# Layer 0 of a two-layer convolution block: chains on GpSimd, edges of t from PSUM, shared statistics, and stores of xs on ScalarE's queue

## The chip, the cores and the metric

The kernel runs on one core of one Trainium2 chip. The metric is the device time of one execution in microseconds; the time of a kernel is the median of its runs. The engines are TensorE (PE; its weight loads are shown as PEld), VectorE (DVE), ScalarE (ACT), GpSimd (POOL) and SyncE (SP, which here only issues DMAs).

## The reference

The input x has 4 images of 64 channels and 256 x 256 pixels in float32. Two layers follow one another, each a residual branch on a group norm:

```python
def _L0_conv_ref(x, ...):
    h = _gelu(_conv2d(x, c1_w, ((1, 1), (1, 1))) + c1_b)          # 3x3, 64 -> 64
    h = _c1x1(h, c2_w, c2_b)                                     # 64 -> 128
    xa, k = jnp.split(h, 2, axis=1)
    xs = _conv2d(xa, sh_w, ((0, 0), (1, 1)), groups=C) + sh_b     # three taps along a row
    xs = _gelu(_conv2d(xs, sv_w, ((1, 1), (0, 0)), groups=C) + sv_b)   # three taps down a column
    pooled = xs.mean(axis=(2, 3))
    weights = jax.nn.softmax(pooled @ gate_w.T, axis=1)          # 3 experts, the top 2 are kept in mask
    ...
    for i, (w1, b1, w2, b2, w3, b3) in enumerate(experts):        # ranks 2, 4, 8
        e = _c1x1(_c1x1(k, w2, b2) * _c1x1(xs, w1, b1), w3, b3)
        out = out + e * mask[:, i][:, None, None, None]           # out starts as xs
    return _c1x1(out, proj_w, proj_b)

def _L1_conv_ref(x, ...):
    h = jax.nn.relu(_batchnorm(_conv3x3(x, _quantize_weight(w1), b1)))
    h = _batchnorm(_conv3x3(h, _quantize_weight(w2), b2))
    return jax.nn.relu(h + x)

x = x + _L0_conv_ref(_gn(x), ...)      # layer 0
x = x + _L1_conv_ref(_gn(x), ...)      # layer 1
```

The batch norms take their mean and variance over all four images, so each convolution of layer 1 has to finish before its norm can be applied. The gate of an image needs the mean of xs over the whole image, so an image's output can't begin before its last rows have passed.

## The kernel before, in words

The two halves of the partitions hold 64 channels each of different rows. Layer 0 works on units: one unit is 16 rows of one image, an image has 16 units, and there are 64 units in all. A unit is worked on in stages, spread over several slots. A slot is the stretch in which one unit's convolution is computed, and there are 64 slots and three tail slots.

In slot u the following happens.

- SP loads x of unit u+3. ACT and GpSimd make row differences of x for units u+2 and u+1 (x_four, x_seconds, v_inner, v_outer; lines 526 to 575), which serve as a row transform of the 3x3 convolution.
- PE multiplies unit u's rows into PSUM (ps_c, line 492). ACT copies parts of it out (mc, L605), DVE combines them in eight butterflies (L610 to L629), and ACT applies the Gelu, which gives h (L637).
- For units u-2 and u-1, PE applies the 1x1 convolution and the column taps together into ps_a, of which there is a single buffer. ACT writes t, the middle tap of the row taps with its bias (`front_taps_i`, L677); DVE adds the left and the right tap, both read from PSUM (`front_taps_h`, L683 and L686), and subtracts from the first and the last column what the padding must not contribute (`ends`, L689). ACT applies the second Gelu, which gives xs and its sums for the pooled mean (`front_xs`, L705), and SP stores xs to DRAM (`xs_store`, L710), 0.5 MB each.
- Every second slot, PE makes the low-rank products (`front_k`, `front_q`), DVE multiplies them (`front_low`, L746), and SP stores them right behind it in program order (L747).

Three further streams share the slots. The statistics of image b+1 are gathered while image b is worked on: a piece of the input is loaded (L409), ACT makes its sum and its sum of squares with two activations (`stats_piece`, L432). For image 0, which comes ahead of all slots, half of the pieces go through DVE's bn_stats instead (`stats_group`, L414), and only the other half through ACT. The statistics of image 1 lie in slots 1 to 12, of image 2 in 12 to 27, of image 3 in 28 to 43; a chain of small operations ends them (`stats_end`). When an image's xs is whole, a chain of small operations makes its gate and the weights of the output (`gate`). Then the output of image b is made, beginning three slots after the next image begins: loads of the low-rank products (L822), of xs (L812) and of x (y, L803), PE's product ps_o, DVE's addition to y (L848), its statistics for layer 1 (L853), and the store of y (L861). `out_end` closes them with another chain of small operations.

The order of the work on every engine is written out by hand. `at_slot(u, pos, call)` puts a call into slot u at a position between 0 and 12; the calls of all streams are sorted by slot and position, and each engine runs its instructions in that order. Where a chain is a generator, each place in a list advances it by one `yield`. The calls of the tail slots are mapped by the table TAIL into the first steps of layer 1. All DMAs, whichever engine issues them, take their completion semaphores in turn from the same set.

Layer 1 is a pair of 3x3 convolutions (L295 and what feeds it), with the batch norms between them, and an end loop (L1422 to L1424) that loads, adds and stores the output. The change doesn't touch it.

Of the kernel before, what the change touches and what calls it, by code (L numbers as in the profile page):

```python
# [41 lines left out]
def conv_preact_kernel(ctx: ExitStack, tc: tile.TileContext, io, col128, colset, col64):  # L42
# [96 lines left out]
    end, ends = column("end", 2), column("ends", 2)  # L139
# [34 lines left out]
    def weights():  # L174
# [22 lines left out]
        nc.vector.tensor_scalar(ends, end, sv_sum, None, ALU.mult)  # L197
        for i in range(2):
            o = outer[:, i, :]
            nc.vector.tensor_scalar(o, zeros[:, 0:W], sh_bias, None, ALU.add)  # L200
            nc.vector.tensor_tensor(o[:, 0 : W : W - 1], o[:, 0 : W : W - 1], end, ALU.subtract)
            nc.vector.tensor_scalar(o, o, c128("sv")[:, 2 * i : 2 * i + 1], None, ALU.mult)
# [59 lines left out]
    def combine(mv, n, avg, eps_t, out, name):  # L262
# [6 lines left out]
        nc.vector.tensor_scalar(mean, mean, 1.0 / n, None, ALU.mult)  # L269
        d = stat.tile([P, n], F32, tag="cd", name=f"d_{name}")  # L270
        nc.vector.tensor_scalar(d, mv[:, :, 0], mean, None, ALU.subtract)
        nc.vector.tensor_tensor(d, d, d, ALU.mult)
        nc.vector.tensor_tensor(d, d, mv[:, :, 1], ALU.add)
# [11 lines left out]
    def group_norm(st, avg, out, name):  # L285
# [3 lines left out]
        yield from combine(mv, 1, avg, eps, out, name)  # L289
# [135 lines left out]

    def stats_piece(b, n, i, at_sum=None):
# [7 lines left out]
    def stats_sums(b, mv):  # L434

        s = stat.tile([P, 2], F32, tag="st_sum", name=f"st_sum_{b}")
        n = NCH if b == 0 else 2 * NCH
        nc.vector.tensor_reduce(s, st_x.pop(b)[:, :, 0:n], AX.X, ALU.add)
        nc.vector.tensor_scalar(s, s, 1.0 / (n * 2 * GF), None, ALU.mult)
        sq = stat.tile([P, 1], F32, tag="st_sq", name=f"st_sq_{b}")  # L440
        nc.vector.tensor_tensor(sq, s[:, 0:1], s[:, 0:1], ALU.mult)
        nc.vector.tensor_tensor(mv[:, 1:2], s[:, 1:2], sq, ALU.subtract)
        nc.vector.tensor_tensor(mv[:, 0:1], s[:, 0:1], shift_x.pop(b), ALU.subtract)
# [12 lines left out]
    def stats_end(b):  # L456

        own = gn1[b] = stat.tile([P, 3], F32, tag="gn1", name=f"gn1_{b}")
        n = 2 if b == 0 else 1
        mv = stat.tile([P, n, 2], F32, tag=f"mv{n}", name=f"mv_x{b}")  # L460
        if b == 0:
            nc.vector.bn_aggr(mv[:, 1, :], flat(st_g.pop(b)))
        stats_sums(b, mv[:, 0, :])
        yield
        yield from combine(mv, n, c128("avg4"), eps, own, f"x{b}")
        if b == 0:
            scale_weights(b)
        nc.vector.tensor_tensor(gn1[b][:, 2:3], gn1[b][:, 0:1], gn1[b][:, 1:2], ALU.mult)
# [204 lines left out]
    def front_taps_i(u, sub):  # L673
# [3 lines left out]
        nc.scalar.activation(flat(t), flat(ps), AF.Identity, bias=tap_bias, scale=sh[:, 1:2])  # L677

    def front_taps_h(u, sub):

        ps = open_a.pop((u, sub)).rearrange("p a b c -> p (a b) c")
        t = open_t[u, sub]
        nc.vector.scalar_tensor_tensor(  # L683
# [4 lines left out]
        )  # L688
        nc.vector.tensor_tensor(  # L689
            t[:, :, 0 : W : W - 1],  # L690
            t[:, :, 0 : W : W - 1],
            ends.unsqueeze(1).to_broadcast([P, 2 * GP, 2]),
            ALU.subtract,
# [13 lines left out]
    def xs_store(u, sub):  # L707
        b, k = divmod(u, NCH)
        n = 2 * k + sub
        nc.sync.dma_start(xs_d[b][:, n, :], flat(xss[b, n]))  # L710
# [32 lines left out]
    def front_low(b, j):  # L743
# [3 lines left out]
        nc.sync.dma_start(low_d[b][:, j, :], low)  # L747
# [4 lines left out]
    def gate(b):  # L752
# [4 lines left out]
        nc.vector.tensor_scalar(spread, zeros[:, 0:P], psum_t, 1.0 / (H * W), ALU.add, ALU.mult)  # L757
# [9 lines left out]
        nc.vector.tensor_scalar(lg, lg, mx, None, ALU.subtract)  # L767
# [8 lines left out]
        yield  # L776
# [3 lines left out]
        nc.vector.tensor_scalar(beat[:, 3:6], beat[:, 0:3], -1.0, 1.0, ALU.mult, ALU.add)  # L780
        keep = stat.tile([P, 3], F32, tag="keep", name=f"keep_{b}")
        for e, (i, j) in enumerate(((3, 4), (0, 5), (1, 2))):
            nc.vector.tensor_tensor(keep[:, e : e + 1], beat[:, i : i + 1], beat[:, j : j + 1], ALU.mult)
        nc.vector.tensor_scalar(keep, keep, -1.0, 1.0, ALU.mult, ALU.add)
        nc.vector.tensor_tensor(keep, g[:, 0:3], keep, ALU.mult)
        yield
# [3 lines left out]
        nc.vector.tensor_tensor(pick[:, 0:4, :], keep.unsqueeze(1).to_broadcast([P, 4, 3]), of, ALU.mult)  # L790
        nc.vector.tensor_tensor(pick[:, 4, :], keep, pb3, ALU.mult)
        row = stat.tile([P, 5], F32, tag="row", name=f"row_{b}")
        nc.vector.tensor_reduce(row, pick, AX.X, ALU.add)
        wm[b] = lstat.tile([P, 4, C], F32, tag="wm", name=f"wm_{b}")
        nc.vector.tensor_tensor(
# [3 lines left out]
        nc.vector.tensor_tensor(out_bias[b], row[:, 4:5], c128("proj_b"), ALU.add)  # L799
# [68 lines left out]
    def out_end(b):  # L868
        gn2[b] = const.tile([P, 3], F32, name=f"gn2_{b}")
        yield from group_norm(st_y.pop(b), c128("avg4"), gn2[b][:, 0:2], f"y{b}")  # L870
        nc.vector.tensor_scalar(gn2[b][:, 2:3], gn2[b][:, 0:1], gn2[b][:, 1:2], -1.0, ALU.mult, ALU.mult)
# [110 lines left out]
    with tc.manual_schedule(engines={mybir.EngineType.Activation}):  # L982
        for k in range(NCH):
# [3 lines left out]
            for i in range({0: 0, NCH - 1: 4}.get(k, 2)):  # L987
                stats_group(0, 2 * k - 2 + i if k else 0, k, i)
            for n in range({0: 2, NCH - 1: 0}.get(k, 1)):
                for i in range(2):  # L990
                    stats_piece(0, 2 * k + n if k == 0 else 2 * k + 1, i, k + n if k == 0 else k + 1)
# [20 lines left out]
    def at_each(places, chain):  # L1012
# [9 lines left out]
        (0, 1.15): (0, 1.15), (0, 1.55): (0, 1.55), (0, 4.7): (0, 4.7), (0, 2): (0, 2), (0, 2.2): (0, 2.2),  # L1022
        (0, 4): (0, 13.2), (0, 4.15): (0, 13.3), (0, 5.2): (0, 13.4), (0, 5.3): (0, 13.5), (0, 8.6): (1, 13.9),
        (0, 9.2): (3, 13.25), (0, 7): (2, 13.2), (0, 7.2): (2, 13.25), (0, 8): (3, 13.1), (0, 9): (3, 13.2), (0, 9.1): (3, 13.3),
        (1, 1.15): (3, 13.4), (1, 1.55): (3, 13.5), (1, 4.7): (4, 13.9), (1, 2): (5, 13.2), (1, 2.2): (5, 13.25),
        (1, 4): (6, 13.2), (1, 4.15): (6, 13.3), (1, 5.2): (6, 13.4), (1, 5.3): (6, 13.5), (1, 8.6): (7, 13.9),
        (1, 8): (8, 13.2), (1, 8.1): (8, 13.3),
# [513 lines left out]
```

## Time and profile before

| | |
|---|---|
| median of 3 runs | 3026.77 us (3007.64 to 3039.1) |
| profiled execution | 3016.92 us |
| its span | 3015.1 us, mean granted TensorE clock 0.913 |
| busy, share of the span | PE 78%, DVE 82%, ACT 68%, POOL 56% |
| layer 0, about | 0 to 1330 us |
| layer 1's two convolutions, about | 1331 to 2564 us |
| end loop, about | 2564 to 3015 us |
| bytes read and written in DRAM | 573.74 MB and 338.17 MB, 302 GB/s over the span |

The lines of a group read: line, engine, operation, output <- inputs by the program's names, shapes, count, then busy time and mean ns of one, then the idle time of the engine just before these instructions and what ended it. A wait line reads: the engine and the line that waits, what released it, the time waited in total, how often, and the longest. A queue with the letter q behind its engine, as SPq, is the stream of DMA issues of that engine. Idle time of an engine that isn't the limit costs nothing.

### The profile page before, as it was taken

What the parts mean: (1) busy time and instruction counts of PE and PEld (TensorE: products, weight loads), DVE (VectorE), ACT (ScalarE), POOL (GpSimd) and SP (SyncE); (2) the same over time, 40 slices, a digit from 0 to 9 for tenths busy, and PEclk for the clock granted to TensorE, in tenths of its full rate; (3) what the DMA queues carried; (4) which work ended last, traced back from release to release, by engine and by line L of the source; (5) the groups of instructions that cost most, each with busy time, mean ns of one, the idle gap of its engine ahead of it and who ended that gap; (6) DMA issues with size and microseconds to landing.
All of it is one profiled execution on the core that took longest, in us unless ns stands there. A gap on an engine that the chain in (4) does not pass through costs nothing.

```text
span 3015.1 us, 52987 instructions
## 1 busy us (share of the span) xinstructions
PE 2357.4 (78%) x21576; PEld 1503.4 (50%) x21576; DVE 2478.0 (82%) x2793; ACT 2054.8 (68%) x2274; POOL 1676.3 (56%) x1210
## 2 busy tenths in 40 slices
PE   1898899998999999988999999989999999000000
PEld 1444444444544445546666667867888888000000
DVE  5678688888888999968988989979999898876665
ACT  6898887787876555557667667868888887422222
POOL 5888887776877778744445546635555555000000
PEclk9999999999999999998999999989999999555555
DMA  8565479999999879848999897746777764899999
GB/s 345 191 249 224 184 259 376 350 342 352 336 343 324 303 288 326 293 147 310 366 356 352 321 345 300 267 178 255 263 266 264 265 232 144 351 411 409 421 427 409
DMA packets 135572, 915.35 MB, mean 304 GB/s; under 512 B 14944, under 2 KB 15712, under 8 KB 40608
## 3 DMA queue, kind: packets, MB, share of 16 engines
q1 hardware_dynamic: 126112, 844.85, 75.0%
q10 hardware_dynamic: 9216, 67.11, 5.5%
q8 instruction: 169, 2.77, 0.4%
q14 instruction: 75, 0.61, 0.1%
HBM read 573.74 MB, written 338.17 MB: 302 GB/s over the span
## 4 chain that ended last, share of the span: by engine, by line
PE 28%; DMA 18%; DVE 5%; issue 2%; ACT 1%; POOL 0%; SPq 0%; DVEq 0%; ACTq 0%; POOLq 0%
PE ps_h L295 18%; PE ps_h2m L295 6%; DMA y_end<-y_d 5%; DMA h<-h_d 4%; DMA out<-h 4%; PE ps_hm L295 3%; DMA y<-in_xp 2%; DVE diff L352 1%; PE ps_o L492 1%; DMA y_d<-y 1%; DVE h L317 1%; DMA h_d<-h 1%; DMA yn<-y_d 1%; DMA xs_in<-xs_d 1%; DVE odd L361 1%
## 5 line engine op out<-in xcount | busy, mean ns | idle before, releaser
L295 PE MATMUL ps_h<-diff,w_q 128*128 128x512 f32 x3072 | 753.8, 400 | 14.3 <-DVE h L317 13.7
L295 PEld LDWEIGHTS ps_h<-diff,w_q 128*128 128x128 f32 x3072 | 576.6, 189 | 192.1 <-issue 23.7
L492 PE MATMUL ps_c<-v,us 64*64 64x256 f32 x9216 | 544.6, 385 | 42.2 <-DVE ps_c L623 36.4
L342 POOL TENSOR_TENSOR d<-yn 128x1024 f32<-128x1024 f32 x128 | 356.0, 2801 | 305.3 <-DMA yn<-y_d 188.5
L492 PEld LDWEIGHTS ps_c<-v,us 64*64 64x64 f32 x9216 | 361.3, 136 | 200.4 <-DVE ps_c L623 45.6
L342 POOL TENSOR_TENSOR d<-h 128x1024 f32<-128x1024 f32 x127 | 311.9, 2477 | 194.8 <-DVE diff L350 133.4
L492 PE MATMUL ps_a<-h,av 64*64 64x512 f32 x4080 | 386.8, 492 | 34.8 <-DVE t L686 23.9
L317 DVE SCALAR_TENSOR_TENSOR h<-ps_h,scale_w,m 128x1024 f32<-128x1024 f32 x256 | 322.8, 1279 | 76.6 <-PE ps_h L295 53.9
L540 POOL TENSOR_TENSOR x<-x 128x512 f32<-128x512 f32 x256 | 329.9, 1289 | 12.3
L1422 ACT ACTIVATE v<-y_end,shift,gn 128x2048 f32<-128x2048 f32 x64 | 133.8, 2092 | 285.1 <-DMA y_end<-y_d 249.9
L492 PEld LDWEIGHTS ps_a<-h,av 64*64 64x64 f32 x4080 | 154.2, 133 | 302.6 <-issue 195.6
L381 ACT ACTIVATE junk<-h,less_h 128x2048 bf16<-128x2048 f32 (+3 forms) x133 | 256.0, 1925 | 11.1 <-DVE h L317 11.0
L1423 DVE SCALAR_TENSOR_TENSOR h<-h,ss,v 128x2048 f32<-128x2048 f32 x64 | 149.8, 2349 | 126.1 <-ACT v L1422 102.1
L683 DVE SCALAR_TENSOR_TENSOR t<-ps_a,m,t 128x1020 f32<-128x1020 f32 x128 | 163.3, 1276 | 103.1 <-ACT t L677 101.1
L848 DVE SCALAR_TENSOR_TENSOR y<-ps_o,ob,y 128x1024 f32<-128x1024 f32 x128 | 163.7, 1279 | 80.6 <-DMA y<-in_xp 27.4
L677 ACT ACTIVATE t<-ps_a,tap_bias,m 128x1024 f32<-128x1024 f32 x128 | 154.0, 1203 | 97.5 <-PE ps_a L492 96.9
L705 ACT ACTIVATE xs<-t 128x1024 f32<-128x1024 f32 x128 | 134.9, 1054 | 116.8 <-DVE t L689 86.8
L352 DVE SCALAR_TENSOR_TENSOR diff<-d,gn,diff 128x1024 fp32r<-128x1024 f32 x128 | 208.5, 1658 | 0.3 <-ACT diff L345 0.3
L295 PE MATMUL ps_hm<-odd,w_q 128*128 128x512 f32 x768 | 194.0, 402 | 8.6 <-ACT m L311 6.0
L295 PE MATMUL ps_h2m<-odd,w_q 128*128 128x512 f32 x768 | 193.2, 400 | 8.2 <-DVE odd L361 4.4
L345 ACT ACTIVATE diff<-d 128x1024 fp32r<-128x1024 f32 x128 | 135.1, 1055 | 83.4 <-POOL d L342 82.2
L532 POOL TENSOR_TENSOR x<-x,x 128x512 f32<-128x512 f32 x128 | 160.7, 1278 | 43.3 <-ACT x L526 43.3
(226 smaller groups left out, 4306.5 us busy)
## 6 DMA issues: line engine op xcount, KB each, us to landing
x<-in_xc SPq DMA_DIRECT2D x64, 1280.0 KB
h<-h_d SPq DMA_DIRECT2D x64, 1152.0 KB
yn<-y_d SPq DMA_DIRECT2D x60, 1152.0 KB
xs_in<-in_xp SPq DMA_DIRECT2D x64, 1024.0 KB
xs_d<-xs SPq DMA_DIRECT2D x128, 512.0 KB
xs_in<-xs_d SPq DMA_DIRECT2D x64, 1024.0 KB
y<-in_xp SPq DMA_DIRECT2D x64, 1024.0 KB
y_d<-y SPq DMA_DIRECT2D x64, 1024.0 KB
```

Of the source, the lines that this page charges most:

```text
L295: nc.tensor.matmul(ps, wq[w][:, kind, kx, :], t[:, rows, kx : kx + W], start=(j == 0), stop=(j == len(terms) - 1))
L317: nc.vector.scalar_tensor_tensor(h.rearrange("p (e k) w -> p e (k w)", e=2), ps.rearrange("p e k w -> p e (k w)"), w_scale[w], m.unsqueeze ...
L342: engine.tensor_tensor(raw.rearrange("p (g r) w -> p g r w", g=2), *pair, ALU.subtract)
L352: nc.vector.scalar_tensor_tensor(lower, raw, scale, upper.bitcast(F32), ALU.mult, ALU.subtract)
L381: nc.scalar.activation(junk[rows, 0:n], flat(h), AF.Square, bias=less[name][rows], accum_out=total)
L492: last[:] = [nc.tensor.matmul(ps[o, at_out[0] : at_out[1], :], w[i], rhs[i], **flags)]
L532: nc.gpsimd.tensor_tensor(x4[:, j - 1], x_rows(u, j + 2), x4[:, j - 1], ALU.subtract)
L540: nc.gpsimd.tensor_tensor(x[:, r : r + 2], x[:, r + 2 : r + 4], x[:, r : r + 2], ALU.subtract)
L677: nc.scalar.activation(flat(t), flat(ps), AF.Identity, bias=tap_bias, scale=sh[:, 1:2])
L683: nc.vector.scalar_tensor_tensor(t[:, :, 1:W], ps[:, :, 0 : W - 1], sh[:, 0:1], t[:, :, 1:W], ALU.mult, ALU.add)
L848: nc.vector.scalar_tensor_tensor(y, ps.rearrange("p x s w -> p x (s w)"), out_bias[b], y, ALU.add, ALU.add)
L1423: nc.vector.scalar_tensor_tensor(h, h, ss2[:, 0:1], v, ALU.mult, ALU.add)
```

## The change

The change has five parts, all in layer 0.

1. **Edges of t.** ACT writes only the inside columns of t. DVE makes the two edge columns first, from PSUM with a bias of their own (`edge_bias`), and then adds the taps. The subtraction of `ends` is gone.
2. **xs stores.** ACT issues them instead of SP, at other positions: (u, 1.6) and (u, 6.135) in place of (u, 4.7) and (u, 8.6).
3. **low store.** It is separated from `front_low` and put at the end of the odd slots, (u, 11.9), behind the store of y at (u, 8.25).
4. **Small operations.** Those of `stats_end` of images 1 to 3, of `gate` of images 0 to 2 and of `out_end` of images 0 and 1 go from DVE to GpSimd where they can; reductions and reciprocals stay on DVE. The square root and the exponential on ACT stand later in their slot, the gate's chain has one more `yield` and ends one slot later, and the output of an image begins four slots after the next image instead of three.
5. **Statistics of image 1.** They are made as those of image 0: half of the pieces by DVE's bn_stats, half by ACT.

The diff, with repeated places of the same kind left out:

```diff
+        nc.vector.tensor_scalar(edge_bias, ends, -1.0, tap_bias, ALU.mult, ALU.add)
...
-    def combine(mv, n, avg, eps_t, out, name):
+    def combine(mv, n, avg, eps_t, out, name, engine=nc.vector):
...
         nc.vector.tensor_reduce(mean, ps[:, 0:n], AX.X, ALU.add)
-        nc.vector.tensor_scalar(mean, mean, 1.0 / n, None, ALU.mult)
+        engine.tensor_scalar(mean, mean, 1.0 / n, None, ALU.mult)
...
+    HALVED = (0, 1)
+
+    def stats_parts(k):
+
+        groups = [(2 * k - 2 + i if k else 0, k, i) for i in range({0: 0, NCH - 1: 4}.get(k, 2))]
+        pieces = [
+            (2 * k + n if k == 0 else 2 * k + 1, k + n if k == 0 else k + 1)
+            for n in range({0: 2, NCH - 1: 0}.get(k, 1))
+        ]
+        return groups, pieces
...
-        nc.scalar.activation(flat(t), flat(ps), AF.Identity, bias=tap_bias, scale=sh[:, 1:2])
+        inside = slice(1, W - 1)
+        nc.scalar.activation(t[:, :, inside], ps[:, :, inside], AF.Identity, bias=tap_bias, scale=sh[:, 1:2])
...
+        edges = slice(0, W, W - 1)
+        nc.vector.scalar_tensor_tensor(
+            t[:, :, edges], ps[:, :, edges], sh[:, 1:2],
+            edge_bias.unsqueeze(1).to_broadcast([P, 2 * GP, 2]), ALU.mult, ALU.add,
+        )
         nc.vector.scalar_tensor_tensor(
             t[:, :, 1:W], ps[:, :, 0 : W - 1], sh[:, 0:1], t[:, :, 1:W], ALU.mult, ALU.add
         )
...
-        nc.vector.tensor_tensor(
-            t[:, :, 0 : W : W - 1], t[:, :, 0 : W : W - 1],
-            ends.unsqueeze(1).to_broadcast([P, 2 * GP, 2]), ALU.subtract,
-        )
...
-        nc.sync.dma_start(xs_d[b][:, n, :], flat(xss[b, n]))
+        nc.scalar.dma_start(xs_d[b][:, n, :], flat(xss[b, n]))
...
-        nc.sync.dma_start(low_d[b][:, j, :], low)
+        low_of[b, j] = low
+
+    def low_store(b, j):
+        nc.sync.dma_start(low_d[b][:, j, :], low_of.pop((b, j)))
...
+        gate_engine = nc.gpsimd if b < B - 1 else nc.vector
+        gate_engine.tensor_scalar(spread, zeros[:, 0:P], psum_t, 1.0 / (H * W), ALU.add, ALU.mult)
...
-                at_slot(u, 8.6, xs_store, u - 2, 1)
+                at_slot(u, 6.135, xs_store, u - 2, 1)
...
-                at_slot(u + 1, 4.7, xs_store, u - 1, 0)
+                at_slot(u + 1, 1.6, xs_store, u - 1, 0)
...
+                at_slot(u, 11.9, low_store, *divmod(j, NOCT // 4))
...
-                places = (t + 1, 8.3), (t + 2, 1.25), (t + 2, 1.36), (t + 2, 1.52), (t + 2, 6.15), (t + 2, 8.3), (t + 2, 9.06)
+                places = (t + 1, 8.3), (t + 2, 1.25), (t + 2, 1.36), (t + 2, 4.45), (t + 2, 6.15), (t + 2, 8.3), (t + 3, 4.1), (t + 3, 4.9)
...
-            for i in range(2):
+            groups, pieces = stats_parts(k) if b in HALVED else ([], [(2 * k, None), (2 * k + 1, None)])
...
+            for group in groups:
+                s = slots[k] + group[2] // 2 * per / 2
+                at_slot(int(s), 4.1 if s - int(s) < 0.5 else 6.2, stats_group, b, *group)
...
-        t = NCH * (b + 1) + 3
+        t = NCH * (b + 1) + 4
...
-            for place in ((e, 8.3), (e + 1, 1.25), (e + 1, 1.36), (e + 2, 1.25), (e + 2, 1.36), (e + 2, 1.52), (e + 2, 6.15)):
+            for place in ((e + 1, 4.1), (e + 2, 1.25), (e + 2, 1.36), (e + 3, 1.25), (e + 3, 1.36), (e + 3, 4.45), (e + 3, 8.3)):
```

## The prediction

> **What bounds the kernel now.** I read the page's chain first, then the windows cut by stage, then the waits, then groups by form.
>
> ```profile
> PE 28%; DMA 18%; DVE 5%; issue 2%; ACT 1%; POOL 0%; SPq 0%; DVEq 0%; ACTq 0%; POOLq 0%
> ```
>
> The chain ends in layer 1, which is the same instructions in both kernels (1331 to 3015 us). So the question is when the front ends, at about 1330 us in the profiled execution. Its windows (columns: stretch and length, then busy us and count of PE, PEld, DVE, ACT, POOL; granted clock; DMA share; GB/s):
>
> ```profile
> 76.00:372.00 296.00, 256.40 (x3676) 136.16 (x3669) 207.87 (x267) 259.34 (x379) 250.42 (x228) 0.97 0.58 211
> 372.00:712.00 340.00, 318.45 (x4445) 163.41 (x4446) 285.69 (x372) 265.54 (x375) 264.54 (x245) 0.99 0.90 334
> 712.00:1055.00 343.00, 323.89 (x4512) 167.68 (x4512) 302.64 (x404) 242.19 (x326) 261.37 (x240) 1.00 0.92 329
> 1118.00:1267.00 149.00, 148.64 (x2120) 77.23 (x2116) 134.58 (x166) 86.92 (x109) 122.66 (x114) 1.00 0.88 313
> ```
>
> Four stages with different limits. Image 0 (first row, about 16 slots): ACT, PE and POOL are each 85 to 88% busy and DMA is at 0.58, so three engines hand work round and ACT is the fullest. Images 1 and 2: DMA at 0.90 to 0.92 with PE at 94%. Last row: PE 148.64 of 149 us; nothing but fewer matmuls shortens it.
>
> From the events at which DMAs complete I worked out more. A 1 MB DMA has 16 completions; 12 come 5 to 9 us after its issue and four, always the same, after 13 to 20 us. From slot 18 to slot 61 those four follow one another without a gap (2.47 us per MB, 1.24 per half). So these slots are paced by four DMA rings: 40.3 to 40.7 us per pair of slots while statistics loads run. Slot lengths, from Gelu to Gelu at L637: slots 2 to 12 mean 17.9, 13 to 18 mean 19.5, 20 to 43 mean 20.3, 44 to 51 between 18.7 and 25.6, 52 to 60 about 18.5.
>
> The queue of SP and the engines wait as follows (waited for: us in total, times, longest):
>
> ```profile
> SPq L803 <- DMA y_d<-y: 372.6, 56, 13.1
> SPq L747 <- DVE k L746: 225.1, 30, 12.4
> SPq L710 <- ACT xs L705: 183.6, 33, 11.5
> SPq L409 <- DMA xs_in<-xs_d: 21.8, 11, 2.1
> ```
> ```profile
> DVE t L683 <- ACT t L677: 101.1, 72, 9.2
> ACT xs L705 <- DVE t L689: 86.8, 50, 3.9
> DVE y L848 <- DMA y<-in_xp: 27.4, 9, 4.5
> PE ps_a L492 <- DVE t L686: 23.9, 27, 3.3
> ```
>
> SP stands 409 us at the stores of xs and low, with loads queued behind. The fourth line is of another kind: a load waiting for a store that it has no data from. The kernel's DMAs share eight completion semaphores in turn, so each issue waits until the DMA eight issues earlier has landed.
>
> The groups that the change touches (times, busy us, mean ns):
>
> ```profile
> L432 ACT ACTIVATE xs_in<-xs_in,shift 128x1024 f32<-128x1024 f32 x112 | 127.1, 1135 | 1.8 <-DVE shift L423 1.8
> L432 ACT ACTIVATE xs_in<-xs_in 128x1024 f32<-128x1024 f32 x112 | 117.9, 1053 | 1.7
> L689 DVE TENSOR_TENSOR t<-t,ends 128x8 f32<-128x8 f32 x128 | 55.2, 431 | 4.4
> L414 DVE BATCH_NORM_STATS2 st_x<-xs_in 128x6 f32<-128x512 f32 x32 | 20.5, 684 | 18.9 <-DMA xs_in<-in_xp 18.9
> ```
>
> **What the skill says.** "SBUF — State Buffer", Who interferes with whom: a DVE instruction with two SBUF inputs contends with a GpSimd instruction that reads SBUF; with at most one, outside the two-port modes, it doesn't. The trace agrees: L689 (both inputs SBUF) takes 172 to 1329 ns, median 269, while L686 (one input PSUM) takes 1280. "GPSIMD Engine Reference", Elementwise — side-by-side cycle accounting: dispatch is about 156 ns on DVE and more hops on GpSimd; POOL's smallest operation here, the L485 memset, takes 0.10 us and its 128x4 and 64x256 ones 278 and 920 ns, so I price a moved operation at 0.3 us. "DMA: Bandwidth & Descriptors", Issuing engines are not separate DMA queues: DMAs of any engine interleave on the same 16 DMA engines, and a second issuer saves only issuing time. Nothing here shows stores from ACT in the front; ACT's store of h_d in layer 1 costs 0.33 us beside a running activation.
>
> **The change part by part.**
>
> *Image 1's statistics.* ACT loses 16 pieces of two activations: 16 x (1.135 + 1.053) = 35 us, plus up to 6 of readouts. DVE gains 32 x 0.684 = 21.9 us. This lies in slots 1 to 12, where DVE has 30% free. ACT's load falls by 35/12 = 2.9 us a slot; behind it stand POOL (4 x 1.29 + 2 x 1.28 + 6 x 1.285 = 15.4, with the memset 15.6 us a slot) and PE (about 15.5). I take 17.9 to 16.2: 12 x 1.7 = -20. Bounds: -28 (down to 15.6), and -8 if DVE's extra 1.8 us a slot stands ahead of the taps.
>
> *Edges of t.* 128 subtractions of mean 431 ns (55.2 us) go; 128 edge operations from PSUM of about 0.18 us come ahead of the two taps. ACT's xs starts 0.25 us earlier, worth something where that wait ends a slot, in slots 13 to 19: -2. Against it, the single PSUM bank of ps_a comes free 0.18 us later, on 27 waits of PE: 5 us at most, all hidden in ring-paced slots.
>
> *xs stores on ACT.* 128 issues of 0.33 us, mostly beside the activation ahead: at nothing, 42 us of ACT if the cover goes. Bytes stay the same. SP no longer waits 184 us for xs, so its loads, and the y_d store behind low, go earlier. In slots 20 to 43 the rings are full, so earlier issues only queue: -4 (from -25, if turn-around gaps fill, to +20, if ACT is held). The new wait: each store on ACT waits for the DMA eight issues before. Counting the new order, in odd slots the first store waits for the y load of the slot before and the second for its y_d store; in even slots both wait for xs stores. Queued behind on ACT are the copies mc, h and t, for which DVE's butterflies and PE wait.
>
> *low store.* Moved behind y_d: SP's 225 us at low no longer hold y_d, so y_d lands some 4 us earlier every second slot, and the y load with it. That and the free SP act where slots stall above PE's 18.55 us: slots 44 to 51, excess 15.1 us in sum, of which I take -9 (-3 to -13). At the end of the front (1305 to 1375) SP stands at xs stores from 1323 to 1345 and at low until 1357, ahead of layer 1's loads; PE has 20 us idle from 1300 to 1400. I take -4 (-10 to +5).
>
> *Small operations on GpSimd.* 9 per later image, about 12 per gate, 5 per out_end: some 70 operations, 0.3 us each, 20 us of POOL, spread where POOL is 75% busy and rings pace. DVE loses its collisions (0.9 to 1.1 us for L757, L767, L775, L780). Nothing, +-5; one chain's end comes a few us later and out of an image starts one slot later. Out then runs into one more tail slot: +2.
>
> Sum: -20 - 2 - 4 - 9 - 4 + 2 = -37 against the profiled 3016.92 us (span 3015.1), so 2980. The four executions known average 3022.6 us, the median of runs is 3026.77; carrying 3022.6 - 37, I give **2985**.
>
> **The rivals.**
>
> *B: given back.* Image 0 ends 20 us sooner, but out of image 0 and the rings come in at the same pace, and image 0's gain is spent waiting: for: from slot 18 four rings have no gap, and the same bytes have to pass. Against: at slots 0 to 17 they have gaps, so earlier bytes are really earlier. -10: 3012.
>
> *C: ACT held by its own stores.* Place: the first xs store of odd slots, behind the y load's landing, 13 to 20 us after an issue that lies less than a slot (20 us) earlier. For: the slow rings land just then, and SPq L409 shows such a wait at 2 us even with SP's looser order. Against: ACT is 70% busy in those slots and can catch up. Price: it decides from 37/21 = 1.8 us per odd slot lost over some 21 odd slots; at 3.3 us it costs 69, a sum of +32: 3055.
>
> *D: faster still.* A second issuer keeps the rings fed, filling turn-arounds and bringing slots 20 to 43 near 19: another -30: 2955. For: PE's floor is 18.55. Against: no gaps are seen in the four slow rings.
>
> **How the numbers follow.** Forecast 0.50, B 0.27, C 0.15, D 0.08. About 1% (30 us) is what a measurement of this kernel can tell from no change, given runs from 3008 to 3039. Faster by over 1% (below 2996) takes the forecast and D: 0.58; within 1% B: 0.27; slower C: 0.15. The range from 2945 to 3040 takes in the forecast's bounds (stage terms all low give some -80, all high +5), D, B and the near side of C.
>
> **What would show it.** Right: slots 2 to 12 near 16.2 us and ACT's share in 76 to 372 lower by about 35 us of work; wait ACT xs behind L689 gone; SPq no longer at xs; the front ending about 1295; layer 1's length unchanged within 5 us. Wrong: ACT waiting at xs's store line for DMA y or y_d, with h and mc late and PE's gaps at ps_c longer in odd slots (C); slots 20 to 43 longer than 20.3 by what image 0 gained (B). If PE's granted clock in layer 1 differs, that part is no work of the change.

## The result, and the profile after

| | before | after |
|---|---|---|
| median | 3019.15 us (6 runs, 3007.64 to 3039.1) | 2988.34 us (6 runs, 2982.45 to 2997.53) |
| ratio | | 0.9903, 95% interval 0.9884 to 0.9922 |
| span of the profiled execution | 3015.1 us | 2988.7 us |

The forecast was 2985 us, and the median lies within 4 us of it. The stages agree less well: in the two profiled executions those of the table below add up to -20.7 us, where the forecast had -37, and two of its terms were wrong altogether. The rest of this text is mostly about those two.

The lengths of the stages, from the start of the first Gelu of each unit (the h activation, one per slot) in the two traces. An eviction is the step with which DVE takes finished products out of PSUM, and conv1 is layer 1's first convolution; the last column is the end of the front, where the last units of layer 0 and the beginning of conv1 overlap.

| us | to slot 13 | 13 to 19 | 20 to 43 | 44 to 51 | 52 to 62 | slot 63 to 16th eviction of conv1 |
|---|---|---|---|---|---|---|
| before | 237.2 | 135.5 | 486.9 | 163.5 | 204.8 | 118.4 |
| after | 236.0 | 129.9 | 480.2 | 156.6 | 206.3 | 116.6 |
| forecast of the difference | -20 | -2 | -4 | -9 | +2 | -4 |
| measured | -1.2 | -5.6 | -6.7 | -6.9 | +1.5 | -1.8 |

The stretch from the last matmul of the second convolution to the end was 446.0 us before and 440.8 after. It is the same instructions in all 14 kernels of this case, and in the 12 others it lies between 440.0 and 443.6 us but for one at 452.9, with 441.2 in a kernel that differs from the one before in a single part; so I take these 5 us for scatter and not for work of the change. About 21 of the 26.4 us by which the two spans differ are then the change's; the medians differ by 30.8 us.

The windows of the changed kernel, with the columns as in the prediction:

```profile
76.00:372.00 296.00, 254.47 (x3712) 135.96 (x3716) 216.74 (x292) 229.62 (x317) 254.94 (x241) 0.98 0.58 212
372.00:712.00 340.00, 322.76 (x4538) 168.91 (x4534) 280.08 (x363) 272.79 (x383) 274.70 (x272) 0.99 0.92 339
712.00:1055.00 343.00, 325.79 (x4533) 167.16 (x4532) 286.67 (x373) 242.73 (x324) 270.13 (x277) 0.99 0.93 327
```

In the first row ACT went from 259.34 to 229.62 us: the 30 us of relief are there. PE's 254.47 is what it was (256.40), so about the same work took the same time with an idler ACT. In the next two rows PE has 2 to 4 us more busy time in the same stretch and the DMA share rose by 0.01 to 0.02, which fits stages that move faster.

The waits of SP's queue and of the engines in the changed kernel:

```profile
SPq L886 <- DVE y L873: 518.2, 64, 22.8
SPq L828 <- DMA y_d<-y: 275.1, 59, 12.8
SPq L770 <- DVE k L764: 214.0, 31, 37.3
```
```profile
ACT xs L723 <- DVE t L710: 88.4, 51, 3.9
PE ps_a L506 <- DVE t L710: 40.1, 36, 3.4
```

SP no longer waits for xs. It now stands longer at the store of y, for DVE's addition. The same wait in the kernel before:

```profile
SPq L861 <- DVE y L848: 282.4, 42, 22.6
```

The wait at low kept its size (225.1 us before), but it now comes behind the store of y. The y load's wait for that store fell from 372.6 to 275.1 us. The wait of ACT's xs for DVE has a new releaser and the old size (86.8 before): the edges are now ahead of the taps, and ACT waits for the last tap instead. PE's wait for the taps grew from 23.9 to 40.1 us.

The edges themselves, and the statistics:

```profile
L699 DVE SCALAR_TENSOR_TENSOR t<-ps_a,m,edge_bias 128x8 f32<-128x8 f32 x128 | 29.1, 227 | 117.0 <-ACT t L692 116.8
L415 DVE BATCH_NORM_STATS2 st_x<-xs_in 128x6 f32<-128x512 f32 x64 | 40.9, 681 | 19.0 <-DMA xs_in<-in_xp 19.0
```

The edge operation takes 227 ns from PSUM where the SBUF subtraction had a mean of 431. There are 64 bn_stats now, 32 of them for image 1.

### The profile page after: what moved, and what is told of

The parts are those of the page before. It is cut to its first block, busy times and chain, and to the rows that moved or that the text cites. A ratio compares the mean times of both kernels' runs of the same rounds, so it can differ in the third digit from the quotient of the medians.

```text
span 2988.7 us, 52829 instructions
## 1 busy us (share of the span) xinstructions
PE 2351.9 (79%) x21576; PEld 1500.3 (50%) x21576; DVE 2440.1 (82%) x2754; ACT 2024.8 (68%) x2210; POOL 1682.5 (56%) x1283
## 4 chain that ended last, share of the span: by engine, by line
PE 50%; DMA 27%; DVE 10%; POOL 6%; ACT 3%; issue 3%; SPq 0%; ACTq 0%; DVEq 0%; POOLq 0%
PE ps_h L296 19%; PE ps_c L506 8%; PE ps_a L506 6%; PE ps_h2m L296 6%; DMA y<-in_xp 6%; DMA y_d<-y 5%; PE ps_o L506 5%; DMA y_end<-y_d 5%; DMA out<-h 4%; DMA h<-h_d 4%; PE ps_hm L296 3%; POOL x L554 2%; DMA xs_in<-xs_d 2%; DVE y L873 1%; DVE t L707 1%
## 5 line engine op out<-in xcount | busy, mean ns | idle before, releaser
L506 PE MATMUL ps_c<-v,us 64*64 64x256 f32 x9216 | 538.4, 382 | 28.6 <-DVE ps_c L637 23.8
L343 POOL TENSOR_TENSOR d<-yn 128x1024 f32<-128x1024 f32 x128 | 347.8, 2738 | 305.6 <-DMA yn<-y_d 189.8
L506 PE MATMUL ps_a<-h,av 64*64 64x512 f32 x4080 | 388.0, 494 | 55.2 <-DVE t L710 40.1
L692 ACT ACTIVATE t<-ps_a,tap_bias,m 128x1016 f32<-128x1016 f32 x128 | 153.4, 1199 | 128.7 <-PE ps_a L506 99.7
L873 DVE SCALAR_TENSOR_TENSOR y<-ps_o,ob,y 128x1024 f32<-128x1024 f32 x128 | 163.9, 1280 | 74.8 <-PE ps_o L506 26.8
L353 DVE SCALAR_TENSOR_TENSOR diff<-d,gn,diff 128x1024 fp32r<-128x1024 f32 x128 | 192.3, 1531 | 0.5 <-ACT diff L346 0.5
L546 POOL TENSOR_TENSOR x<-x,x 128x512 f32<-128x512 f32 x128 | 160.9, 1280 | 22.2 <-ACT x L540 22.2
L296 PEld LDWEIGHTS ps_h2m<-odd,w_q 128*128 128x128 f32 x768 | 146.3, 191 | 44.5 <-DVE odd L362 5.2
```

The costliest lines, as they stand in the source:

```text
L296: nc.tensor.matmul(ps, wq[w][:, kind, kx, :], t[:, rows, kx : kx + W], start=(j == 0), stop=(j == len(terms) - 1))
L343: engine.tensor_tensor(raw.rearrange("p (g r) w -> p g r w", g=2), *pair, ALU.subtract)
L353: nc.vector.scalar_tensor_tensor(lower, raw, scale, upper.bitcast(F32), ALU.mult, ALU.subtract)
L506: last[:] = [nc.tensor.matmul(ps[o, at_out[0] : at_out[1], :], w[i], rhs[i], **flags)]
L546: nc.gpsimd.tensor_tensor(x4[:, j - 1], x_rows(u, j + 2), x4[:, j - 1], ALU.subtract)
L692: nc.scalar.activation(t[:, :, inside], ps[:, :, inside], AF.Identity, bias=tap_bias, scale=sh[:, 1:2])
```

## The experiments

Twelve kernels ran, in three groups of four. A ratio is against runs of the kernel before in the same group (its median was 3018.91, 3014.01 and 3016.73 us in the three). Multiply a difference of ratios by 3017 for microseconds. The intervals are about +-0.0018 wide, so the difference of two variants is uncertain by some 0.0025, or 8 us; smaller differences are read from the stage table further down or not at all. A stage is read from one profile, and slots 20 to 43 scatter by several us there.

### Statistics of image 1 back on ScalarE

```diff
-    HALVED = (0, 1)
+    HALVED = (0,)
```

> The changed kernel with image 1's statistics all on ScalarE again (the halving for image 0 alone); the other four parts stay. My prediction gave this part -20 us: by it the time is 3008 and slots 2 to 12 go from 16.2 to 17.9 us. The trace of the changed kernel says otherwise: its slots 2 to 12 are still about 17.8 us, because the two bn_stats that DVE now makes (1.2 to 1.4 us) stand in the loop PE ps_c, ACT mc, four DVE butterflies, two bn_stats, DVE edges and taps, PE ps_a, PE ps_k, PE ps_c, of 17.7 us. By that theory what ACT gains DVE's loop takes, and undoing the part costs 0 to 5 us: 2988 to 2993. Rival: GpSimd bounds these slots, whatever ACT and DVE do: the same 0 here.

Measured: 2984.88 us, ratio 0.9885 (0.9867 to 0.9903). Undoing the part costs nothing that can be seen (the ratio is 0.0018 lower, not told apart from 0); a loss of 20 us would have been a ratio of 0.9969, far outside the interval. ACT was busy 186.52 of 200 us between 110 and 310 here and 154.92 in the changed kernel, and the stage to slot 13 is 235.9 against 236.0 us. The -20 is refuted.

### bn_stats behind the taps

```diff
-                at_slot(int(s), 4.1 if s - int(s) < 0.5 else 6.2, stats_group, b, *group)
+                at_slot(int(s), 5.25 if s - int(s) < 0.5 else 6.2, stats_group, b, *group)
```

> The changed kernel with the first two of each slot's bn_stats for image 1 placed behind the taps of t (position 5.25) instead of ahead of them (4.1). Loop theory: the loop shortens by the 1.2 us that the trace's chain shows for them, slots 2 to 12 go from 17.7 to 16.5, and the time by some 12 us to 2976. Rival (GpSimd, 15.6 us of work and a wait of about 2 us for its tick in each slot, or PE is the bound): slots stay at 17.7 and the time at 2988.

Measured: 2986.42 us, ratio 0.9891 (0.9873 to 0.991). Slots 2 to 10 are at 17.1 to 17.9 us and the stage at 235.4. The loop theory in this form fell: the bn_stats had been on the chain, but taking them off it saved 0.6 us in thirteen slots, not 12. The chain then ran through GpSimd (v, v, v, 2.0 us idle, tick), which made GpSimd the next suspect.

### GpSimd's tick one operation later

The tick is a memset on GpSimd that waits for one group of PE's products in ps_a and releases the next.

```diff
-                at_slot(u, 2.2, divide)
+                at_slot(u, 2.35 if u < UNITS else 2.2, divide)
...
-                at_slot(int(s), 4.1 if s - int(s) < 0.5 else 6.2, stats_group, b, *group)
+                at_slot(int(s), 5.25 if s - int(s) < 0.5 else 6.2, stats_group, b, *group)
```

> The changed kernel with bn_stats behind the taps (as in the run with position 5.25) and with GpSimd's tick of the first half of a slot (L499, a memset that orders two groups of PE's products in ps_a) one GpSimd operation later: position 2.35 instead of 2.2. Theory now: slots 2 to 12 are GpSimd's, 15.4 us of work and 2.0 us in which it stands at the tick for PE's products, 17.4 in sum; with the tick behind v (1.22 us) it stands 0.8 us and a slot takes 16.5 us, the length of the PE, DVE loop. Image 0 gets shorter by some 10 us and the time falls to 2976. Rival: what image 0 gains is spent in the ring-paced slots that follow: slots 2 to 12 at 16.5 but 2986 as before. Second rival: PE waits longer for the later tick and the slots stay at 17.4.

Measured: 2983.96 us, ratio 0.9901 (0.9883 to 0.9919). GpSimd's idle time ahead of the tick fell from 2.0 to 0.8 us as expected, and slots 2 to 10 stayed at 17.1 to 17.7. The chain of waits of this run helps to see why; the longest pieces of one period (start, length, what):

```profile
138.87 1.30 POOL v L581
140.25 1.27 POOL v L582
141.53 1.25 POOL v L584
142.78 0.79 issue
143.59 0.11 POOL tick L499
143.74 0.71 PE ps_a L506 x8
144.47 1.21 ACT t L692
145.70 0.24 DVE t L699
145.97 1.29 DVE t L707
147.29 1.29 DVE t L710
148.58 0.14 issue
148.72 2.38 PE ps_a L506 x24
151.10 1.88 PE ps_k L737 x32
152.97 0.59 PE ps_a L506 x8
153.56 1.35 PE ps_c L506 x22
154.99 1.29 POOL v L580
156.28 1.31 POOL v L581
```

From v to v it is 156.28 - 138.87 = 17.41 us, and all four engines appear. One piece has to be read with care, the 0.79 us of "issue" ahead of the tick. The waits of this run from 110 to 310 us put GpSimd's idle time there down to PE:

```profile
POOL tick L499 <- PE ps_a L506: 11.6, 10, 5.6
```

PE was at work without a break from 136.0 to 143.5 us (ps_c, then ps_a), and the tick waited for the end of this. So the v operations run beside PE, and only the tick itself, 0.11 us, is on the loop that ends last. Moving it shortened GpSimd's idle time and nothing else, and the theory that these slots are GpSimd's falls.

What remains is PE's own row and what it waits for. From 143.74 to 148.72 us PE makes the last products of one half, ACT writes t from them, and DVE adds the edges and the taps; the single buffer of ps_a keeps PE from the next half until then, and it has only 2.8 us of ps_c to do meanwhile. The next half, ps_k and ps_a follow without a gap, then ps_c. In these 17.41 us PE works 15.7 and stands 0.9 us for the taps, 0.6 for DVE's butterflies (ps_c) and 0.3 for the tick. None of these three waits ends with an operation of the statistics.

The same waits of PE from 110 to 310 us, first before, then in the changed kernel:

```profile
PE ps_c L492 <- DVE ps_c L623: 15.9, 12, 2.2
PE ps_a L492 <- POOL tick L485: 3.6, 13, 0.4
PE ps_a L492 <- DVE t L686: 1.8, 3, 0.7
```
```profile
PE ps_a L506 <- DVE t L710: 14.0, 12, 1.9
PE ps_c L506 <- DVE ps_c L637: 7.2, 12, 0.7
PE ps_a L506 <- POOL tick L499: 2.8, 11, 0.3
```

With 30 us less on ACT, PE's wait for the butterflies fell from 15.9 to 7.2 us, and its wait for the taps rose from 1.8 to 14.0. In sum PE waited 21.3 us before and 24.0 after. In the run with image 1's statistics back on ACT the two waits are 12.1 and 7.4 us, so a good part of this shift is the relief's and the rest that of the other parts; with the tick they make 22.5 us, between the two sums. The prediction had taken the fullest engine for the bound, and the floors per engine (15.6 and 15.5 us) for what comes next. What a second buffer of ps_a would do was not tried.

### xs stores on SyncE again

```diff
-        nc.scalar.dma_start(xs_d[b][:, n, :], flat(xss[b, n]))
+        nc.sync.dma_start(xs_d[b][:, n, :], flat(xss[b, n]))
...
-                at_slot(u, 6.135, xs_store, u - 2, 1)
+                at_slot(u, 8.6, xs_store, u - 2, 1)
...
-                at_slot(u + 1, 1.6, xs_store, u - 1, 0)
+                at_slot(u + 1, 4.7, xs_store, u - 1, 0)
```

> The changed kernel with the xs stores issued by SyncE again, at their places of before; low stays behind y_d. My prediction gave the stores and the low store together -17 us in slots 20 to 51 and at the end of the front; if most of this is the stores', the time is about 3001, with slots 20 to 43 longer than now. Rival: the 15 us in which ACT is held at its stores (t behind y and y_d) come back, and the time falls to about 2975. Second rival: the queue of the store makes no difference (bytes and rings are the same): 2988.

Measured: 3004.76 us, ratio 0.9953 (0.9936 to 0.997). Undone, this costs 0.0050, or 15 us. ACT is no longer held at its stores here, and the time rose all the same, so the first rival falls. In its profile, 5.4 us of it lie in slots 20 to 43 (485.6 against 480.2) and 2.8 us at the end of the front. Over all profiles the end is clearer: in the three with xs stores on SP (before, this one, and the chains alone) the 16th eviction of the first convolution comes 118.4, 119.4 and 118.7 us after slot 63's Gelu, and in the eleven with the stores on ACT 111.4 to 116.6. The rest isn't located; a single profile can't place it.

### low stored at once again

```diff
...
-                at_slot(u, 11.9, low_store, *divmod(j, NOCT // 4))
+                at_slot(u, 8.15, low_store, *divmod(j, NOCT // 4))
```

> The changed kernel with the low store issued right behind its product again (position 8.15, ahead of y_d's store at 8.25). My prediction: SP held at low makes y_d and the next y load some 4 us late in every second slot; undone, a third to half of the 13 us of slots 44 to 51 and of the front's end go: 2993 to 2995. Rival 1: this is the larger part of the change's gain, since the y loop is the longest SP wait: 3000 or more. Rival 2: the rings set the pace and nothing moves: 2988.

Measured: 2993.8 us, ratio 0.9916 (0.9897 to 0.9934): 4 us on the time, which the ratio can't tell from 0, and 9.5 in slots 20 to 43 of its profile (489.7 against 480.2). Slots 44 to 51, where I had put most of this store's gain, did not grow (154.9 against 156.6 in the changed kernel). What ACT waits for in the front, first in the changed kernel, then in this one:

```profile
ACT t L692 <- DMA y_d<-y: 9.4, 3, 3.5
ACT t L692 <- DMA y<-in_xp: 5.9, 1, 5.9
```
```profile
ACT t L692 <- DMA y<-in_xp: 23.7, 6, 4.8
ACT t L692 <- DMA y_d<-y: 15.0, 5, 3.7
```

ACT's t reads nothing that these DMAs bring. What stands ahead of it is the store of xs, which waits for the completion of the DMA eight issues before. This is the wait of rival C: 15 us in the changed kernel (one of the four waits behind the y load, which rival C named, and three behind the y_d store), 39 with the early low store. It suggests a way of paying that I hadn't seen: behind low, y_d and y go out later and land later, and with them ACT comes free later. How much of the 9.5 us comes from ACT and how much from the later loads isn't shown.

### The small operations on VectorE again

```diff
-        small_engine = nc.vector if b == 0 else nc.gpsimd
+        small_engine = nc.vector
...
-        gate_engine = nc.gpsimd if b < B - 1 else nc.vector
+        gate_engine = nc.vector
```

and likewise in `combine`, `gn1` and `gn2`.

> The changed kernel with the chains' small operations on VectorE again, at the places of the changed kernel. My prediction: 0 +-5 us, 2983 to 2993. Theory from the traces: the kernel before had PE standing 4.1 us at ps_m_y behind the gate's pick on DVE in slots 34 and 50, and those slots took 25.0 and 25.6 us; the changed kernel has 19.2 and 18.7. If this is the engine's doing, undoing it brings 6 us back in each of the slots 34 and 50 and some in 13 to 19: 3000 to 3005. Rival: it is the new places (output one slot later), and the engine makes no difference: 2988.

Measured: 2992.67 us, ratio 0.993 (0.9911 to 0.9949): 0.0027, or 8 us, where the theory had 12 to 17. Slot 50 is back at 25.4 us, slot 18 goes from 16.0 to 19.2 and slot 34 from 19.2 to 22.2, while slot 46 falls from 23.3 to 19.1. The 8 us are at the edge of what two ratios can tell; the slots are clearer. PE's longest wait from 1030 to 1075 us, around slot 50, is now for DVE's taps:

```profile
PE ps_a L506 <- DVE t L710: 5.4, 2, 3.6
```

The engine matters, and in one chain it does harm.

### Chains and output at their places of before

```diff
...
-        t = NCH * (b + 1) + 4
+        t = NCH * (b + 1) + 3
...
-            for place in ((e + 1, 4.1), (e + 2, 1.25), (e + 2, 1.36), (e + 3, 1.25), (e + 3, 1.36), (e + 3, 4.45), (e + 3, 8.3)):
+            for place in ((e, 8.3), (e + 1, 1.25), (e + 1, 1.36), (e + 2, 1.25), (e + 2, 1.36), (e + 2, 1.52), (e + 2, 6.15)):
```

and likewise the places of `gate` and `stats_end`.

> The changed kernel with the output of an image beginning three slots after the next image again, and the chains at their places of before (the gate's added step right behind the last); the engines stay GpSimd. If the stalls of slots 34 and 50 (25.0 and 25.6 us before, 19.2 and 18.7 after) come from the chains of gate and out_end meeting, they return: 6 us each, 3000. Rival: with the small operations on GpSimd the chains are short enough wherever they stand: 2986 to 2988, 2 us less for the tail slot that the output no longer enters.

Measured: 2996.45 us, ratio 0.9941 (0.9919 to 0.9962): 0.0038, or 11 us. The stages 13 to 19 and 44 to 51 go back to 136.1 and 163.6 us, those of the kernel before. Its profile was the fastest of its six runs (2985.83 us), with short slots 20 to 43, so the 11 us rest on the medians and not on this profile. In slot 50 (and likewise in slot 34) PE stands at a small product of out_end, for a reduction of the gate that stays on DVE; from 1030 to 1075 us:

```profile
PE ps_m_y L267 <- DVE row L817: 2.0, 1, 2.0
```

So GpSimd without the new places brings nothing in the lengths of these two stages, and the new places without GpSimd a part only (134.1 and 160.8): both are needed.

### Edges of t the old way

```diff
...
-        nc.scalar.activation(t[:, :, inside], ps[:, :, inside], AF.Identity, bias=tap_bias, scale=sh[:, 1:2])
+        nc.scalar.activation(flat(t), flat(ps), AF.Identity, bias=tap_bias, scale=sh[:, 1:2])
...
-        nc.vector.scalar_tensor_tensor(
-            t[:, :, edges],
...
+        nc.vector.tensor_tensor(
+            t[:, :, 0 : W : W - 1],
...
```

> The changed kernel with the edges of t made the old way: ScalarE writes all columns, DVE subtracts the ends behind the taps. My prediction gave this part -2 us: 2990. Rival: the 128 subtractions of mean 0.43 us and up to 1.33 us are the reason for the gain in slots 13 to 19 (6.5 us, the same in every variant so far): 2995. Second rival: the edge operation ahead of the taps holds the single bank of ps_a 0.2 us longer twice a slot, on the path where PE sets the pace, and undoing it gains: 2980.

Measured: 2988.84 us, ratio 0.9912 (0.9891 to 0.9933). 0.0009 is 3 us, the size of the forecast's 2, and not told apart from 0. The rival that gave it the gain of slots 13 to 19 falls: that stage is 129.1 us here and 129.9 with the new edges.

### The chains alone

The changed kernel with the four other parts undone, by the edits above.

> Of the five parts of the change only the chains' (small operations on GpSimd, their places, the output one slot later); statistics, edges, the xs stores and low are as in the kernel before. My prediction: 0 +-5 and +2 for the tail slot, 3019. Theory from the undoing runs (engines 7.5 us, places 11 us): these two are the same stalls, at slots 18 and 19, 34 and 50, seen twice or added; the part alone brings 10 to 18 us against the kernel before, 3001 to 3009.

Measured: 2999.68 us, ratio 0.9947 (0.9929 to 0.9965): 16 us, half of the whole gain, from the part that I had priced at 0 +-5. The four other parts together make the rest, 0.9947 - 0.9903 or 13 us. The stages 13 to 19 and 44 to 51 are 129.3 and 157.4 us, 6 us less each than before; 20 to 43 is 485.2, only 1.7 less, though slot 34 lost its stall (19.2 instead of 25.0). My reading is that where the rings (the slow completions of the prediction) set the pace, the other slots spend what one slot saves; no run tests this.

### xs stores on ScalarE alone

The kernel before with the edits of the xs stores in the other direction.

> The kernel before with only the xs stores moved to ScalarE's queue, at the changed kernel's places. Undoing this in the changed kernel cost 16 us. Theory: the store's place in SyncE's queue is what costs, and alone the part brings 10 to 16 us, 3003 to 3009. My prediction gave both stores 17 us together. Rival: it pays only beside the other parts, since SyncE still stands at low: 3015 or more.

Measured: 3019.08 us, ratio 1.0011 (0.9995 to 1.0026). Alone the part brings nothing, although undoing it costs 15 us. The time is the rival's, and SP, free of xs, stands longer at low, as it had said. Its wait there from 372 to 1290 us (slot 16 on), first before, then here:

```profile
SPq L747 <- DVE k L746: 158.5, 22, 12.4
```
```profile
SPq L747 <- DVE k L746: 198.0, 22, 23.4
```

Slots 20 to 43 take 496.2 us, 9.3 more than before; slots 13 to 19 take 5.5 more, and the front's end gives some back (113.2 against 118.4). The stage table shows the two stores as a pair in slots 20 to 43: the five kernels with one or both at the old place take 485.2 to 496.2 us there, the nine with both moved 472.9 to 480.6. The front's end follows the xs stores alone. The medians don't show the pair as clearly, since undoing low alone cost only 4 us; low moved alone was not run.

### A version without the one harmful chain

In the changed kernel's slot 46 (from 961.7 us on) GpSimd stands at a small operation of `stats_end`, and PE at ps_a for the tick that is queued behind it; waits of the changed kernel from 958 to 984 us:

```profile
POOL gn L482 <- DVE gn L284: 2.9, 1, 2.9
PE ps_a L506 <- POOL tick L499: 2.4, 1, 2.4
```

```diff
-        small_engine = nc.vector if b == 0 else nc.gpsimd
+        small_engine = nc.vector
...
-        yield from combine(mv, n, c128("avg4"), eps, own, f"x{b}", nc.vector if b == 0 else nc.gpsimd)
+        yield from combine(mv, n, c128("avg4"), eps, own, f"x{b}", nc.vector)
...
-        product = nc.vector if b == 0 else nc.gpsimd
+        product = nc.vector
```

> The changed kernel with only the small operations of stats_end on VectorE again; those of gate and out_end stay on GpSimd. In the changed kernel's slot 46 (23.3 us) GpSimd stands 2.9 us at the product gn (L482) for DVE's reciprocal, its tick comes that much later, and PE stands 2.4 us at ps_a for the tick; with all small operations on VectorE that slot took 19.1. Theory: slot 46 goes to 19.1 and slot 30 loses 1 to 2 us, in sum 5 to 6 us, about 2982. Rival: the rings take it back in the same slots: 2988.

Measured: 2977.82 us, ratio 0.9874 (0.9856 to 0.9892). Slot 46 is at 19.1 us and slot 30 at 19.7 (21.9 in the changed kernel). This is the fastest kernel of the case by its median; its interval overlaps that of the changed kernel (0.9884 to 0.9922) at the edge, so it is the two slots, 6.4 us together, more than the ratio that show the gain. With bn_stats and the tick later as well:

> The run before it, and bn_stats behind the taps and the tick one operation later. Each of these two alone left slots 2 to 12 at 17.4 us. Theory: those slots stay there, and the sum is that of the run before it, 2980 to 2982; together with the two runs so far (2986, 2984) this would be the fastest version. Rival: 2988, no difference from the changed kernel.

Measured: 2978.44 us, ratio 0.9872 (0.9849 to 0.9895): the same, as expected of two edits that each left slots 2 to 12 alone.

The stages of all kernels, one profile each (us):

| kernel | to slot 13 | 13 to 19 | 20 to 43 | 44 to 51 | ratio |
|---|---|---|---|---|---|
| before | 237.2 | 135.5 | 486.9 | 163.5 | 1 |
| xs stores alone | 235.9 | 141.0 | 496.2 | 163.9 | 1.0011 |
| chains alone | 238.6 | 129.3 | 485.2 | 157.4 | 0.9947 |
| changed | 236.0 | 129.9 | 480.2 | 156.6 | 0.9903 |
| without ACT's relief | 235.9 | 129.9 | 478.1 | 156.5 | 0.9885 |
| bn_stats behind taps | 235.4 | 130.7 | 480.6 | 156.6 | 0.9891 |
| tick later | 236.4 | 128.3 | 474.4 | 156.3 | 0.9901 |
| without xs stores on ACT | 236.1 | 130.1 | 485.6 | 155.3 | 0.9953 |
| low early | 235.8 | 129.9 | 489.7 | 154.9 | 0.9916 |
| small operations on DVE | 235.8 | 134.1 | 478.3 | 160.8 | 0.993 |
| places of before | 235.9 | 136.1 | 473.3 | 163.6 | 0.9941 |
| old edges | 237.6 | 129.1 | 477.1 | 157.4 | 0.9912 |
| stats_end on DVE | 235.9 | 129.9 | 473.9 | 152.4 | 0.9874 |
| the same, bn_stats and tick later | 235.9 | 129.3 | 472.9 | 152.3 | 0.9872 |

## Why the prediction was right, and where it was not

**Image 1's statistics, -20: wrong.** The failed step is "I take 17.9 to 16.2". ACT's share was read rightly and the relief came, but ACT's load didn't set the length of slots 2 to 12. PE has 15.7 to 15.9 us of products in each of them (slots 2 to 10; the prediction had 15.5) and stands another 1.9 to 2.0 us, in the kernel before and in the changed one. The relief moved part of this wait from the butterflies to the taps, where PE waits for ACT's t and DVE behind the single buffer of ps_a. Three edits, aimed at ACT, DVE and GpSimd in turn, left the stage within 1 us of 236. The lower bound of -8 was too sure as well: it allowed for DVE's share of the work, not for the case that ACT was no bound at all.

**Small operations on GpSimd, 0 +-5: wrong.** Alone the part, with its places and the later output, measured -16 us. The kernel before had told it in a place that I priced otherwise. Waits of the kernel before from 1060 to 1100 us:

```profile
PE ps_m_y L266 <- DVE pick L791: 4.1, 1, 4.1
```

PE stood 4.1 us at the small product of out_end, behind the gate's operations on DVE, and in the same stretch ACT's mc waited up to 6.6 us and GpSimd's v up to 5.6 us for PE. The same wait, of the same length, is in slot 34. These two slots were the longest of their stages (25.0 and 25.6 us). I had slot 50 in the sum, in the "excess 15.1 us" of slots 44 to 51, but put it down to SP's late y_d and charged -9 to the low store. The size of that term was near (6.9), which was luck, for its cause was another: with the low store early again the stage is still 154.9 us, and with the chains' old places it is 163.6. A wait on PE that holds a whole stage should have been followed by name before the excess was shared out.

**xs and low stores, -17 with the front's end: near in size, not in place.** The -9 of slots 44 to 51 belongs to the chains. In slots 20 to 43 the step "the rings are full, so earlier issues only queue" gave too little: the nine kernels with both stores moved take 39.4 to 40.1 us a pair of slots, less than the 40.3 to 40.7 that I had read as the rings' pace. Their mean is 476.5 us for the stage, and the two kernels with both stores at the old place take 485.2 and 486.9, so the gain is about 10 us where I had -4. The front's end was right, about -5 over the profiles. By the medians the xs stores cost 15 us undone and the low store 4, and these don't add: all parts but the chains make 13 us together. That the two stores depend on each other wasn't in the forecast: the xs stores alone measured 1.0011.

**Rival C, the hold on ACT: real, too small to decide.** It costs 15 us of ACT's time in four places, or 0.7 us for each of some 21 odd slots, where it would decide from 1.8. Rival B wasn't tested: image 0 had no gain to give back. Nothing speaks for rival D at -67.

**Edges, -2, and the tail slot, +2:** 3 us by the ratio, not told apart from 0, and 1.5 us by the stage.

So the time was right with luck. The -20 wasn't there, and what came in its place is the chains' -16, of which some 6 us lie in slots 44 to 51 and had been counted under another name, and more than forecast from the stores. In the two profiles this makes up a part only (-20.7 of -37); the medians came nearer, -30.8, and the starting value of 3022.6 lay 3.5 us above the later median.

Of the signs, "slots 2 to 12 near 16.2" failed at once, and so did "ACT xs behind L689 gone": that wait moved to the last tap with its size. "SPq no longer at xs" came. The front did not end 35 us sooner, as 1295 in place of about 1330 meant: the first product of the first convolution came at 1291.7 us in place of 1308.4, 17 us sooner, and its 16th eviction 20 us sooner. Layer 1 was to keep its length within 5 us; from that first product to the end it took 1706.7 us before and 1697.0 after, but between 1688.7 and 1707.9 in the 14 profiles, so this sign could not have told anything.

## What to carry to other kernels

Where three or four engines are each 85 to 88% busy, relief of the fullest one may shorten nothing. Take an engine whose instructions fill most of the stage in order (here PE), list what it waits for, and ask whether a shorter wait at one place comes back at another: here 15.9 us for the butterflies became 7.2, and 1.8 us for the taps became 14.0. Where a chain of waits has a piece called "issue", look among that engine's waits for its releaser before reading it as the engine's own time.

Small operations are priced by whom they keep waiting in an in-order queue: moved to a less busy engine, at other places, they took some 6 us off each of two slots, and placed there behind a wait for another engine (here 2.9 us at a 0.2 us product) they made a new stall. A store moved to another queue takes its waits along, so look at what else is still ahead of the loads in the old queue and at what now stands behind the store in the new one.

## What the runs showed of the hardware

On GpSimd the chains' moved operations took 0.19 to 0.38 us each in the changed kernel's profile, but for one of 128x256 with 0.61 (each the mean of 1 to 9). My price of 0.3 us was near. Against their means on DVE before, some took less: the product gn 196 ns (906), keep 192 (415), lg 334 (903), pick 207 (455). Others took more: the scaling of gn 224 (154), the last keep 195 (162), the second pick 196 (150), the 128x256 product 608 (424). So neither engine was the faster one for all of them. DVE's means for similar shapes range from 0.15 to 1.1 us in the same profile; why was not tested.
